# A four-layer graph network on one core: order of the seven products, engine of one product, joined differences, and order at the start of layer 0

## The chip, the cores and the metric

The kernel runs on one core of one Trainium2 chip. A core has engines that each work through their own queue in order: PE (TensorE, the matrix products), DVE (VectorE), ACT (ScalarE), POOL (GpSimd) and SP (SyncE, which here only issues transfers). They meet through semaphores. Matrix products land in PSUM, which this kernel uses as eight banks; everything else lives in SBUF. The metric is the time of one execution in device microseconds (us), and the median of three runs is what versions are compared by.

## The reference

The input `x` has 128 graphs of 64 nodes with 256 features, in float32, and there is one 64x64 adjacency matrix. Four layers follow each other, each `x = x + f(relu(layernorm(x)), adj)`:

```python
# layer 0: two graph convolutions, then an LSTM with windows of 1, 2, 3 and 4 nodes
h = relu(einsum('ts,bsh->bth', adj, x @ Wg0 + bg0))
h = relu(einsum('ts,bsh->bth', adj, h @ Wg1 + bg1))
for p in range(1, 5):                       # own weights for each p
    nw = T // p
    last = lstm_last(Wih[p-1], Whh[p-1], b, h[:, :nw*p].reshape(B*nw, p, H))
    h = h.at[:, arange(nw) * p + (p-1)].set(last.reshape(B, nw, H))
# one LSTM step: g = x_t @ Wih.T + h @ Whh.T + bias; i, f, gg, o = split(g)
#   c = sigmoid(f) * c + sigmoid(i) * tanh(gg);  h = sigmoid(o) * tanh(c)
# layer 1: masked attention; layer 2: graph convolution, two dense layers, batch norm
# layer 3: three times  einsum('nm,bmh->bnh', adj*adj, h @ W)  with relu between
```

In the first step of a window `h` and `c` are zero, so only the product with `Wih` is left and the forget gate isn't needed.

## The kernel before

**Tiling.** The 8192 tokens (graph, node) are cut into 16 groups of 512 (`NG`, tile `[128, 4, 256]`). Adjacency products are done by `mix`: 32 small 64x64 matrix products into two banks, and one copy out of each bank (L146). Wide products in the LSTM and in layer 3 use a scheme of seven half-size products in place of eight.

**Seven products.** `seven` (L153) takes a dictionary of seven products, four banks, and two work tiles `p1` and `p5`. Products 1, 5, 6, 7 go to the four banks; ACT copies the first two banks to `p1` (L162) and `p5` (L163); DVE adds the third bank into `p1` (L165) and the fourth into `p5` (L166). `finish` then lets POOL make block (1,1) from `p1 + p5` (L169), adds product 2 into bank 0 for block (0,0), product 4 into bank 3 for block (1,0), where DVE adds `p1` (L174), and product 3 into bank 1 for block (0,1), where DVE adds `p1` (L177). `end(m, n, ps)` does what follows a block: in the LSTM the gates' activations on ACT (L472), in layer 3 the relu or a copy (L202, L204). In the LSTM `end(1, 0)` acts on both blocks of row 1 at once. Product 4 is added into bank 3 and so comes after that bank's reader, L166; product 3 is added into bank 1 and comes after L163. The operands need sums of one factor's blocks (`sums`, L190) and differences of the other's (`differences`, L182), four instructions each.

**Layer 0, first half.** `first_mix(g)` (L345) normalises group g (`ln_scale`: statistics L91 and L93 on DVE, a power on POOL L95, L97 on DVE; `ln_apply`: L102 on ACT) and mixes it. `first_weights` multiplies with the first weights (L380; DVE adds the bias, L388; POOL's relu, L389), `second_mix` and `second_weights` (L404, L409, L412) follow, as a pipeline over 16 groups. Around the first group stand small setup works: `adjacency_forms` and `normalized_adjacency` on DVE.

**Layer 0, LSTM.** For each window length p the sequences are cut into units; two units are taken together. `first_steps` (L515) does the first time step of both: the differences of each unit's inputs (L184 to L188, 128x256 each), three gate sets with seven products each (input and cell gates of unit 0, output gates of both, input and cell gates of unit 1), then the cell product i * g (`new_cell`, L534, on POOL), its tanh on ACT (L491) and the product with the output gate on DVE (L499, or L493 where another step follows). There are 17 such pairs: 8, 4, 3 and 2 for p = 1 to 4. A gate set's `finish` is put behind the next gate set's first four products by `take`. `next_step` (L549) does the later time steps, a gate set's two halves back to back. The sums of the first-step weights are made by `first_blocks` (L573; L192 to L195 on DVE).

**What sets the order.** The instructions of each engine are put in order when the program is compiled: of those whose operands are ready in a model of the machine, the first in program order is issued next. So order in the source is a wish and not a command. `tc.issue_after(ins)` adds the command that what stands in its block is queued on that instruction's engine behind `ins`, without a wait for it. On the chip each queue is then worked through in that fixed order. All loads of `x` and of the weights go through SP's queue.

Of the kernel before, what the change touches and what calls it, by code (L numbers as in the profile page):

```python
# [8 lines left out]
F32 = mybir.dt.float32  # L9
AF = mybir.ActivationFunctionType  # L10
ALU = mybir.AluOpType
# [3 lines left out]
P = 128  # L15
# [5 lines left out]
NG = NTOK // GN  # L21
GB = GN // NODES
HB = 32
PER = HB // GB
NK = PER
# [13 lines left out]
def adj_preln_kernel(ctx: ExitStack, tc: tile.TileContext, x_in, adj, vec, bg0, bg1,  # L39
                     wg0, wg1, wih, whh, wqkv, w1t, w2t, l3w1, l3w2, l3w3, out):  # L40
    nc = tc.nc
# [111 lines left out]
    def seven(products, banks, p1, p5, out, end):  # L153

        ps = banks
        for i, p in zip((1, 5, 6, 7), ps):  # L160
            products[i](p, True)
        nc.scalar.copy(p1, ps[0])  # L162
        nc.scalar.copy(p5, ps[1])  # L163

        nc.vector.tensor_tensor(p1, p1, ps[2], ALU.add)  # L165
        nc.vector.tensor_tensor(p5, p5, ps[3], ALU.add)  # L166

        def finish():
            nc.gpsimd.tensor_tensor(out=out[1][1], in0=p1, in1=p5, op=ALU.add)  # L169
            end(1, 1, None)  # L170
            products[2](ps[0], False)
            end(0, 0, ps[0])
            products[4](ps[3], False)
            nc.vector.tensor_tensor(out[1][0], p1, ps[3], ALU.add)  # L174
            end(1, 0, None)
            products[3](ps[1], False)
            nc.vector.tensor_tensor(out[0][1], p1, ps[1], ALU.add)  # L177
            end(0, 1, None)

        return finish  # L180

    def differences(eng, b11, b12, b21, b22, t1, t2, t3, t4, negate=False):  # L182

        eng.tensor_tensor(out=t1, in0=b12, in1=b11, op=ALU.subtract)  # L184
        eng.tensor_tensor(out=t3, in0=b22, in1=b12, op=ALU.subtract)
        eng.tensor_tensor(out=t2, in0=b22, in1=t1, op=ALU.subtract)  # L186
        t4a, t4b = (b21, t2) if negate else (t2, b21)
        return eng.tensor_tensor(out=t4, in0=t4a, in1=t4b, op=ALU.subtract).ins  # L188
# [63 lines left out]
    with tc.tile_pool(name="lw", bufs=5) as lw:  # L252
# [6 lines left out]
        with tc.tile_pool(name="gw", bufs=1) as gw, tc.tile_pool(name="gcn", bufs=2) as gp, \  # L259
                tc.tile_pool(name="setup", bufs=1) as sp:  # L260

            load_x(xs[0], 0)
            abd = sp.tile([P, P], F32, tag="abd", name="abd")
            nc.vector.memset(abd, 0.0)
            arow = sp.tile([P, NODES], F32, tag="arow", name="arow")
# [77 lines left out]
            first_copied = None  # L343

            def first_mix(g):  # L345
                nonlocal first_copied
# [24 lines left out]

            def first_weights(m0):
# [52 lines left out]
        with tc.tile_pool(name="back", bufs=1, reuse_waits="tile") as back_pool, \  # L425
                tc.tile_pool(name="diff", bufs=2, reuse_waits="tile") as dp, \
                tc.tile_pool(name="lstm", bufs=2, reuse_waits="tile") as lp:

            def unit(p, tiles, k0, nk):


                n = nk * HB
                win = [
                    hs[i][:, :, k0 * p : (k0 + nk) * p, :].rearrange("p c (k q) b -> p c k q b", q=p)
                    for i in tiles
                ]
                state = lp.tile([P, 2, 2, 2, 256], F32, tag="state", name="state")
                cell, hid = (state[:, i, :, :, 0:n] for i in range(2))
                return lambda t, blk: win[blk][:, :, :, t, :], cell, hid
# [72 lines left out]
                    finish()  # L512
                    then()

            def first_steps(p, n, two, w0):  # L515


                bs = []
                tt = dp.tile([P, 4, 2, 256], F32, tag="diff", name="diff")
                for u, (x_of, _, _) in enumerate(two):  # L520
                    ts = [tt[:, i, u, 0:n] for i in range(4)]
                    x = [[x_of(0, blk)[:, c] for blk in range(2)] for c in range(2)]
                    differences(
                        nc.vector, *x[0], *x[1],
                        *[d.rearrange("p (k b) -> p k b", b=HB) for d in ts], negate=True,
                    )
                    bs.append(([[x[0][0]], None], [[x[1][0]], [x[1][1]]], [[d] for d in ts]))
                igs = [gate_tile() for _ in range(2)]
                both = gate_tile()

                def new_cell(i):
                    def then():
                        gate_i, gate_g = (igs[i][:, r, :, :, 0:n] for r in range(2))
                        nc.gpsimd.tensor_tensor(out=two[i][1], in0=gate_i, in1=gate_g, op=ALU.mult)  # L534
# [12 lines left out]
                take(lambda: gate_set(p, n, igs[1], ig, w0, [bs[1]] * 2), new_cell(1))  # L547
# [43 lines left out]
                return [by_chunk([wx[:, m], wm[:, m]]) for m in range(2)] + [by_chunk(ss)]  # L591


            w0 = first_blocks(w_next[0], lw.tile([P, 2, 1024], F32, tag="w", name="s"))
            for p, nk in ((1, 8), (2, 8), (3, 7), (4, 8)):
                n = nk * HB
                wi, wh = w_next
# [4 lines left out]

                for j in range(0, len(units), 2):
                    two = [unit(p, *u, nk) for u in units[j : j + 2]]
                    first_steps(p, n, two, w0)
                    if p > 1:
                        flush()
                        if j == 0:
# [577 lines left out]
```

## Time and profile before

| what | us |
|---|---|
| runs of this kernel | 2577.28, 2571.56, 2572.81 |
| median of them | 2572.81 |
| the profiled execution | 2576.97 |
| its span in the trace | 2574.9 |
| PE busy in the span | 2492.7 |
| DVE busy | 1457.1 |
| ACT busy | 1132.3 |
| POOL busy | 506.7 |

The span runs from the first to the last instruction; 2.1 us of the profiled execution lie around it. The profiled execution was 4.2 us above the median of the runs. Its mean granted TensorE clock was 0.993. PE's row counts matrix products that overlap, so a mean duration of 370 to 380 ns belongs to products that start about 0.23 us apart (16 of them take 3.73 us on the chain of waits). Every matrix product in the source is two instructions in the trace.

### The profile page before, as it was taken

The page shows a single profiled execution, that of the slowest core. Times are in us where ns is not written, and L with a number is a line of the kernel's source. Part 1 is how long each engine was busy: PE and PEld are TensorE (multiplying, and loading weights), DVE is VectorE, ACT ScalarE, POOL GpSimd, SP SyncE. Part 2 cuts the span into 40 slices and gives each one's busy share as a digit, 9 for nine tenths or more (in the row PEclk, how much of TensorE's full clock was granted, in tenths as well). Part 3 has the DMA queues.
Part 4 walks back from the last instruction along what each step waited for, and adds up shares of the span by engine and source line. Part 5 has one row for each costly group of instructions (what it writes and reads, how often), then busy time and mean ns, then how long its engine had stood idle before and what let it go on. Part 6 is the DMA issues. An engine that isn't in the chain of part 4 may idle for free.

```text
span 2574.9 us, 46812 instructions
## 1 busy us (share of the span) xinstructions
PE 2492.7 (97%) x20184; PEld 2045.8 (79%) x20184; DVE 1457.1 (57%) x2636; ACT 1132.3 (44%) x1982; POOL 506.7 (20%) x384
## 2 busy tenths in 40 slices
PE   6999999999999999999999999998999999999998
PEld 4668778888999998888866664444889889889888
DVE  6547775556555665565466666423645545545544
ACT  3546654444444443344455556472333332332332
POOL 3334432221121121121123221003110110110110
PEclk9999999999999999999999999998999999999999
DMA  4100000001000000000200000001000000000000
GB/s 151 59 2 1 1 17 1 1 1 33 1 1 1 1 1 1 1 29 1 82 2 2 2 18 1 1 21 37 10 9 9 18 10 9 18 9 10 18 9 17
DMA packets 30207, 39.67 MB, mean 15 GB/s; under 512 B 1712, under 2 KB 26416, under 8 KB 30000
## 3 DMA queue, kind: packets, MB, share of 16 engines
q1 hardware_dynamic: 29136, 36.09, 4.2%
q8 instruction: 158, 2.59, 0.4%
q10 hardware_dynamic: 864, 0.59, 0.1%
q14 instruction: 49, 0.40, 0.1%
HBM read 28.29 MB, written 8.39 MB: 14 GB/s over the span
## 4 chain that ended last, share of the span: by engine, by line
PE 80%; DVE 9%; ACT 5%; POOL 3%; issue 2%; DMA 1%; SPq 0%; DVEq 0%; POOLq 0%; ACTq 0%
PE ps L458 29%; PE ps L1010 15%; PE ps L1055 8%; PE ps L690 4%; PE ps L911 4%; PE ps L974 4%; PE ps L134 3%; ACT gates L472 3%; PE ps L663 3%; POOL state L534 2%; PE ps L706 2%; PE ps L380 2%; PE ps L404 2%; ACT gates L491 1%; DVE state L493 1%
## 5 line engine op out<-in xcount | busy, mean ns | idle before, releaser
L458 PE MATMUL ps<-diff,s 128*128 128x256 f32 (+1 forms) x1824 | 397.2, 372 | 13.4 <-DVE diff L561 7.1
L1010 PE MATMUL ps<-arena 128*128 128x256 f32 x1792 | 391.8, 380 | 0.3 <-DVE arena L186 0.2
L458 PEld LDWEIGHTS ps<-diff,s 128*128 128x128 f32 x1824 | 344.8, 190 | 51.6 <-issue 8.9
L1010 PEld LDWEIGHTS ps<-arena 128*128 128x128 f32 x1792 | 338.2, 190 | 53.4 <-issue 7.3
L472 ACT ACTIVATE gates<-gates,lbias 128x512 f32<-128x512 f32 (+4 forms) x426 | 240.5, 619 | 192.1 <-DVE gates L174 166.5
L169 POOL TENSOR_TENSOR gates<-p 128x512 f32<-128x512 f32 (+1 forms) x115 | 154.1, 1340 | 734.0 <-DVE p L166 710.4
L458 PE MATMUL ps<-diff,w 128*128 128x256 f32 (+1 forms) x1040 | 242.0, 374 | 13.5 <-DVE p L166 12.3
L458 PE MATMUL ps<-h,w 128*128 128x256 f32 (+1 forms) x1028 | 241.0, 371 | 0.0
L458 PEld LDWEIGHTS ps<-diff,w 128*128 128x128 f32 x1040 | 196.4, 191 | 37.0 <-DVE p L166 16.4
L458 PEld LDWEIGHTS ps<-h,w 128*128 128x128 f32 x1028 | 194.8, 190 | 18.9 <-issue 0.5
L472 ACT ACTIVATE gates<-ps,lbias 128x256 f32<-128x256 f32 (+3 forms) x213 | 91.4, 476 | 238.3 <-PE ps L458 238.3
L169 POOL TENSOR_TENSOR arena<-arena 128x512 f32<-128x512 f32 x64 | 73.2, 1144 | 540.2 <-DVE arena L166 540.2
L204 ACT ACTIVATE arena<-arena 128x512 f32<-128x512 f32 x144 | 89.4, 630 | 181.5 <-POOL arena L169 103.4
L1055 PE MATMUL ps<-arena 128*128 128x128 f32 x1280 | 153.0, 277 | 1.4 <-DVE arena L192 1.0
L1055 PEld LDWEIGHTS ps<-arena 128*128 128x128 f32 x1280 | 147.0, 192 | 2.9 <-PE ps L1055 1.7
L174 DVE TENSOR_TENSOR gates<-p,ps 128x512 f32<-128x512 f32 (+1 forms) x115 | 76.5, 665 | 119.0 <-PE ps L458 118.6
L165 DVE TENSOR_TENSOR p<-p,ps 128x512 f32<-128x512 f32 (+1 forms) x115 | 76.3, 663 | 101.4 <-PE ps L458 77.1
L174 DVE TENSOR_TENSOR arena<-arena,ps 128x512 f32<-128x512 f32 x64 | 39.8, 621 | 152.2 <-PE ps L1010 84.2
L95 POOL TENSOR_TENSOR rstd<-rstd,mhalf 128x4 f32<-128x4 f32 x64 | 65.4, 1022 | 275.8 <-DVE rstd L94 269.5
L663 PE MATMUL ps<-arena,w 128*128 128x512 f32 x256 | 117.4, 613 | 1.4 <-DVE arena L146 1.3
L458 PE MATMUL ps<-state,s 128*128 128x256 f32 (+1 forms) x512 | 118.0, 374 | 0.0
L458 PE MATMUL ps<-state,w 128*128 128x256 f32 (+1 forms) x512 | 116.0, 370 | 1.4 <-ACT p L162 1.4
(184 smaller groups left out, 4007.7 us busy)
## 6 DMA issues: line engine op xcount, KB each, us to landing
x<-in_x SPq DMA_DIRECT2D x28, 512.0 KB, 5.0
out<-x SPq DMA_DIRECT2D x16, 512.0 KB, 2.9
w<-in_wih SPq DMA_DIRECT2D x4, 1024.0 KB, 9.5
w<-in_whh SPq DMA_DIRECT2D x3, 1024.0 KB, 4.9
arena<-in_l3w SPq DMA_DIRECT2D x3, 1024.0 KB, 5.1
w<-in_wqkv SPq DMA_DIRECT2D x1, 768.0 KB, 4.5
wg<-in_wg ACTq DMA_DIRECT2D x2, 256.0 KB, 3.4
w<-in_w1t SPq DMA_DIRECT2D x1, 512.0 KB, 3.9
```

The source lines that it names most:

```text
L134: nc.tensor.matmul(pss[b][half * 64 : half * 64 + 64, c, t, :], lhsT=src[rows, t, col : col + 64], rhs=a2[rows, :], start=True, stop=True,)
L169: nc.gpsimd.tensor_tensor(out=out[1][1], in0=p1, in1=p5, op=ALU.add)
L174: nc.vector.tensor_tensor(out[1][0], p1, ps[3], ALU.add)
L204: nc.scalar.activation(out[m][n], out[m][n], func)
L458: nc.tensor.matmul(ps[:, r], lhsT=wc[:, j, :], rhs=bc, start=first and r == 0 and c == 0, stop=True, skip_group_check=True,)
L472: nc.scalar.activation(o, ps, func, bias=lbias[:, col : col + 1])
L663: nc.tensor.matmul(ps, lhsT=w1[:, c, m * P : (m + 1) * P], rhs=a[:, 2 + c, :], start=(c == 0), stop=(c == 1),)
L690: nc.tensor.matmul(ps, lhsT=wqk[:, c, col : col + P], rhs=hT[:, c, :], start=(c == 0), stop=(c == 1),)
L911: nc.tensor.matmul(pss[m], lhsT=w2[:, c, m * P : (m + 1) * P], rhs=a[:, c, :], start=(c == 0), stop=(c == 3),)
L974: nc.tensor.matmul(ps[:, t, :], lhsT=w[:, t * P : (t + 1) * P], rhs=b, start=first and t == 0, stop=True, skip_group_check=True,)
L1010: nc.tensor.matmul(ps[:, r, :], lhsT=w[:, c, col : col + P], rhs=b[:, c, :], start=first and r == 0 and c == 0, stop=c == 1, skip_group_ch ...
L1055: nc.tensor.matmul(ps[:, t, :], lhsT=w[:, c, t * P : (t + 1) * P], rhs=b[:, c, :], start=first and t == 0 and c == 0, stop=c == 3, skip_gr ...
```

## The change

Four edits. In `seven`, product 3 and what follows it come before product 4. At the start of layer 0, the load of group 1 is issued right after that of group 0; the statistics of group 1 are queued behind the copies out of group 0's mix, and the setup works and later statistics behind group 1's last statistics instruction; the first call of `first_blocks` is queued behind the copies of group 8's mix. In `first_steps`, the differences of two neighbouring units of the same tiles are made by one set of four instructions over both (two sets remain where the units lie in different tiles, which is the case for one pair of p = 3). The cell product of the first steps goes from POOL to DVE.

```diff
@@ seven @@
             end(0, 0, ps[0])
+            products[3](ps[1], False)
+            nc.vector.tensor_tensor(out[0][1], p1, ps[1], ALU.add)
+            end(0, 1, None)
             products[4](ps[3], False)
             nc.vector.tensor_tensor(out[1][0], p1, ps[3], ALU.add)
             end(1, 0, None)
-            products[3](ps[1], False)
-            nc.vector.tensor_tensor(out[0][1], p1, ps[1], ALU.add)
-            end(0, 1, None)
@@ layer 0 @@
-            load_x(xs[0], 0)
+            for g in range(2):
+                load_x(xs[g], g)
...
-            for g in range(1, NK):
+            for g in range(2, NK):
                 load_x(xs[g], g)
...
-                    with tc.issue_after(first_ln):
+                    with tc.issue_after(first_copied):
                         rstd, nmr, second_ln = ln_scale(xs[1])
                     ln_apply(xs[1], h, rstd, nmr)
-                    with tc.issue_after(second_ln), tc.issue_after(first_copied):
+                    with tc.issue_after(second_ln):
                         adjacency_forms()
                         normalized_adjacency()
...
-                    with tc.issue_after(first_copied):
+                    with tc.issue_after(second_ln):
                         ln_relu(x, h)
...
+                if g == NG // 2:
+                    middle_copied = copied
@@ first_steps @@
-            def first_steps(p, n, two, w0):
+            def first_steps(p, n, two, places, w0):
...
+                (tiles, k0), (tiles_b, k0_b) = places
+                nk = n // HB
+                if tiles == tiles_b:
+
+                    spans = [(k0, 2 * nk, tiles, slice(0, 2))]
+                else:
+                    spans = [(k0, nk, tiles, 0), (k0_b, nk, tiles_b, 1)]
+                for k, span, tls, u in spans:
+                    x = [[windows(p, i, k, span)[:, c, :, 0] for i in tls] for c in range(2)]
+                    ts = [tt[:, i, u, 0:n] for i in range(4)]
...
+                    differences(nc.vector, *x[0], *x[1], *ts, negate=True)
...
-                        nc.gpsimd.tensor_tensor(out=two[i][1], in0=gate_i, in1=gate_g, op=ALU.mult)
+                        nc.vector.tensor_tensor(out=two[i][1], in0=gate_i, in1=gate_g, op=ALU.mult)
...
-            w0 = first_blocks(w_next[0], lw.tile([P, 2, 1024], F32, tag="w", name="s"))
+            with tc.issue_after(middle_copied):
+                w0 = first_blocks(w_next[0], lw.tile([P, 2, 1024], F32, tag="w", name="s"))
```

More of the change, by code (lines that the diff above doesn't have):

```diff
@@ L338, in adj_preln_kernel @@
                 nc.vector.tensor_scalar(rb0[:, 0, :], rb0[:, 0, :], rsum, None, ALU.mult)
-            for g in range(1, NK):
+            for g in range(2, NK):
                 load_x(xs[g], g)
             w_next = (load_w(wih, 0), None)
-            first_copied = None
+            first_copied, middle_copied, second_ln = None, None, None
             def first_mix(g):
-                nonlocal first_copied
+                nonlocal first_copied, middle_copied, second_ln
                 h = gp.tile([P, GT, D], F32, tag="h", name="h")
@@ L427, in adj_preln_kernel, with windows @@
                 tc.tile_pool(name="lstm", bufs=2, reuse_waits="tile") as lp:
+            def windows(p, i, k0, nk):
+                return hs[i][:, :, k0 * p : (k0 + nk) * p, :].rearrange("p c (k q) b -> p c k q b", q=p)
             def unit(p, tiles, k0, nk):
                 n = nk * HB
[L433 to L436, printed above, removed]
+                win = [windows(p, i, k0, nk) for i in tiles]
                 state = lp.tile([P, 2, 2, 2, 256], F32, tag="state", name="state")
@@ L513, in flush @@
                     then()
-            def first_steps(p, n, two, w0):
+            def first_steps(p, n, two, places, w0):
                 bs = []
                 tt = dp.tile([P, 4, 2, 256], F32, tag="diff", name="diff")
+                (tiles, k0), (tiles_b, k0_b) = places
[7 more added lines that the diff above has]
+                    ts = [tt[:, i, u, 0:n] for i in range(4)]
+                    if span > nk:
+                        x = [[b.rearrange("p (u k) b -> p u k b", u=2) for b in row] for row in x]
+                        ts = [d.rearrange("p u (k b) -> p u k b", b=HB) for d in ts]
+                    else:
+                        ts = [d.rearrange("p (k b) -> p k b", b=HB) for d in ts]
+                    differences(nc.vector, *x[0], *x[1], *ts, negate=True)
                 for u, (x_of, _, _) in enumerate(two):
-                    ts = [tt[:, i, u, 0:n] for i in range(4)]
                     x = [[x_of(0, blk)[:, c] for blk in range(2)] for c in range(2)]
-                    differences(
-                        nc.vector, *x[0], *x[1],
-                        *[d.rearrange("p (k b) -> p k b", b=HB) for d in ts], negate=True,
+                    bs.append(
+                        ([[x[0][0]], None], [[x[1][0]], [x[1][1]]], [[tt[:, i, u, 0:n]] for i in range(4)])
                     )
-                    bs.append(([[x[0][0]], None], [[x[1][0]], [x[1][1]]], [[d] for d in ts]))
                 igs = [gate_tile() for _ in range(2)]
@@ L604, in adj_preln_kernel @@
                     two = [unit(p, *u, nk) for u in units[j : j + 2]]
-                    first_steps(p, n, two, w0)
+                    first_steps(p, n, two, units[j : j + 2], w0)
                     if p > 1:
```

## The prediction

> **What bounds the kernel now.** I read the busy times by stage first. The stages are my cuts: start of layer 0, its steady part, LSTM with p = 1, LSTM with p = 2 to 4, layers 1 and 2, start, body and end of layer 3.
>
> ```profile
> core 0: us, PE busy (x) PEld busy (x) DVE busy (x) ACT busy (x) POOL busy (x), PEclk, DMA share, GB/s
> 0.00:60.00 60.00, 36.74 (x526) 26.13 (x527) 39.01 (x140) 20.78 (x35) 20.04 (x23) 0.96 0.46 163
> 60.00:187.00 127.00, 125.17 (x1916) 83.90 (x1914) 64.28 (x149) 62.63 (x93) 45.73 (x34) 0.99 0.10 31
> 187.00:345.00 158.00, 151.03 (x684) 128.80 (x684) 121.38 (x200) 105.30 (x183) 67.43 (x40) 1.00 0.00 1
> 345.00:1270.00 925.00, 903.69 (x4368) 825.21 (x4367) 551.89 (x766) 411.19 (x759) 176.20 (x116) 1.00 0.02 7
> ...
> 1812.00:2555.00 743.00, 742.44 (x7082) 662.31 (x7081) 370.28 (x681) 242.53 (x438) 86.41 (x77) 1.00 0.04 12
> 2555.00:2575.00 20.00, 12.93 (x120) 12.09 (x119) 7.69 (x10) 1.62 (x4) 0.72 (x1) 0.97 0.08 27
> ```
>
> PE is the bound almost everywhere, and the change takes no matrix product away. So it can only win PE's idle time: 23.3 us in the first 60, 7.0 in p = 1, 21.3 in p = 2 to 4, next to nothing in layer 3's body. What PE waits for there is in the groups of the whole page's list:
>
> ```profile
> L458 PE MATMUL ps<-diff,s 128*128 128x256 f32 (+1 forms) x1824 | 397.2, 372 | 13.4 <-DVE diff L561 7.1
> L458 PE MATMUL ps<-diff,w 128*128 128x256 f32 (+1 forms) x1040 | 242.0, 374 | 13.5 <-DVE p L166 12.3
> L458 PE MATMUL ps<-state,w 128*128 128x256 f32 (+1 forms) x512 | 116.0, 370 | 1.4 <-ACT p L162 1.4
> ```
>
> `diff,w` is product 4, and it waits for L166, the reader of its bank. With 13.4 and 1.4 this makes 28.3 us, the most that the LSTM can give. Third, the timeline of the start:
>
> ```profile
> 10.93 1.07 DVE L91 BATCH_NORM_STATS2 st<-x 128x6 f32<-128x256 f32 x3
> 13.61 0.16 DVE L97 SCALAR_TENSOR_TENSOR nmr<-mv,rstd 128x4 f32<-128x4 f32 x1 [1.12 <-POOL rstd L95]
> 16.22 0.69 DVE L192 TENSOR_TENSOR s<-w 128x512 f32<-128x512 f32 x1 [2.44 <-DMA w<-in_wih]
> 16.83 0.68 DVE L194 TENSOR_TENSOR s<-w 128x512 f32<-128x512 f32 x1
> 17.54 1.29 DVE L146 COPY m<-ps 128x512 f32<-128x512 f32 x2
> 18.89 6.34 PE L380 MATMUL ps<-wg,m 128*128 128x256 f32 x16 [7.37 <-DVE m L146]
> ```
>
> The mix of group 0 was done at 11.52, but its two copies L146 stand in DVE's queue behind the statistics of group 1 and behind two sums of LSTM weights, whose transfer lands at 16.22. Fourth, the timeline where a second time step begins:
>
> ```profile
> 435.43 2.85 POOL L534 TENSOR_TENSOR state<-gates 128x1024 f32<-128x1024 f32 x1 [6.37 <-ACT gates L472]
> 438.31 1.06 ACT L491 ACTIVATE gates<-state 128x1024 f32<-128x1024 f32 x1 [2.07 <-POOL state L534]
> 439.40 1.23 DVE L493 TENSOR_TENSOR state<-gates 128x1024 f32<-128x1024 f32 x1 [3.33 <-ACT gates L491]
> 440.55 0.68 DVE L165 TENSOR_TENSOR p<-p,ps 128x512 f32<-128x512 f32 x1
> 441.74 0.68 DVE L166 TENSOR_TENSOR p<-p,ps 128x512 f32<-128x512 f32 x1
> 442.48 1.99 PE L458 MATMUL ps<-diff,w 128*128 128x256 f32 x8 [1.97 <-DVE p L166]
> ```
>
> One chain: cell product on POOL, tanh, product with the output gate; L165 and L166 of the next gate set queue behind it on DVE; product 4 waits 1.97 us.
>
> **What the Trainium skill says.** "PSUM — Partial Sum Buffer", section "Engine vs sequencer instructions", calls the queues of ScalarE, VectorE and GpSimd strict FIFO. The trace agrees: L146 had its data at 11.52 and began at 17.54. "SBUF — State Buffer", section "Who interferes with whom", says that a DVE instruction with two inputs in SBUF contends with a GpSimd instruction that reads SBUF, and that the second one is fully blocked. The trace agrees: L185 at 230.12 took 2.57 us where its median is 0.418, beside an L534 from 229.93 on that took 2.48. "GPSIMD Engine Reference", section "4.1 Engine selection", puts two-input work on GPSIMD at about twice VectorE's time. Here L534 has a median of 2.367 us, and the same shape on DVE (L493, 128x1024) 1.224.
>
> **Start of layer 0.** With the copies queued ahead of the statistics and the sums gone from there, L146 can start at 11.55 and PE's L380 at 12.9, as 1.35 us lay between the two before. 18.89 - 12.9 is 6.0 us. What is late next: group 1's statistics now follow the copies at 12.85; from L91 to the end of L97 they took from 10.33 to 13.77 with an L338 of 0.34 between, so 3.1 us. h of group 1 then comes out of ACT by 18.2. PE works on L380 till 19.2 if it is as slow there as before (6.34 us), so it doesn't wait. The setup works (2 us from 18.75 to 20.5) now stand behind group 1's L97 at 16 and may sit in front of the first L388: I take 0.5 us off. Group 1's transfer is issued ahead of three small ones (vectors and biases); these are first read at 10.68 (L338, before L388 only), so nothing of them is late. ACT's adjacency transfers share the engines with it: they landed by 5.8, and L279 was done at 7.00 with L97 at 7.84, so 0.8 us are free. The four sums L192 to L195 (4 x 0.68 = 2.7 us) go to about 105 us, where DVE is half busy (64.3 of 127) and PE full; without that cover they would cost 2.7. **-5.5**, between -1 (another wait at once in its place) and -7 (DVE freed of L193 and L195 as well).
>
> **Cell product.** 34 times 1.224 on DVE in place of 2.367 on POOL: tanh starts 1.14 us earlier each time. In p = 1 PE waits 0.83 us in almost every pair for L472, which stands on ACT behind L491, which waits for L534 (POOL state L534 made ACT idle 57.0 us over all). Of the 6.98 us of p = 1 I take **-5.0**: the waits for L472 are 5.5, those for L174 (0.15 a pair) stay. DVE's load: 121.4 us over 8 pairs is 15.2 of 19.7 a pair; two cell products add 2.45, joined differences take 8 x 0.418 - 4 x 0.683 = 0.6 off (0.683 is L557's and L561's 128x512), and blocked L184, L185, L188 (means 561, 1192, 499 ns against 419, 418, 414) give back 2.0. So 15.1 to 17.1, under 19.7. At the first gate set of p = 1 the joined L184 takes 0.68 in place of 0.42 with PE waiting: **+0.3**. Where a next step follows, L561 stands behind L493 of unit 0, which is behind the same tanh: four waits of 1.35 to 2.02 shrink by 1.1 each (**-4.4**; one of them was an L195 blocked for 2.84 us by L534).
>
> **Third product ahead of the fourth.** Product 3 needs L163 only, done long before; it lasts 1.8 us in a next step (8 instructions at 0.23) and 0.9 in a first one. In the quoted case product 4 comes at 442.3 and L166 is done at 442.3 even without the quicker cell product, at 441.2 with it. So the waits for L166 go: **-11.7** of 12.3. A gate set's last two activations are now 128x512 instead of 128x256 (2.13 of four either way; later by about 0.4 us), hidden in a step, since the other unit's step (26 us of PE) lies between.
>
> **Layer 3.** At the end, L1055's product 5 waited for L192, which needs block (0,1):
>
> ```profile
> 2556.89 4.48 PE L1055 MATMUL ps<-arena 128*128 128x128 f32 x38 [1.01 <-DVE arena L192]
> 2568.45 1.09 PE L1076 MATMUL ps<-arena,w2s 64*64 64x256 f32 x16 [0.61 <-DVE arena L177]
> ```
>
> (0,1) comes one product (1.7 us) earlier, so the 1.01 goes; half of L1076 can start without the 0.61. **-1.5**. In the body it is the other way round: the second mix begins with (0,0) and (1,0), and (1,0) is now last. Before, it was ready at 2099.3 when PE reached it at 2099.4; now L174 and L204 end near 2100.1. PE would wait up to 0.7 us in 15 groups, 10.5 us, unless other matrix products are put there: the half of the mix that reads (0,1), or the second half of L1076 (0.6 us). Since ready work is issued first, I take **+1.0** (0 to 10.5).
>
> **Sum.** -5.5 - 5.0 + 0.3 - 4.4 - 11.7 - 1.5 + 1.0 = -26.8. Against the profiled execution's 2576.97 (span 2574.9 and 2.1 around it) this is 2550.2; that execution lay 4.2 over the median, so from 2572.81 it is 2546.
>
> **Rivals.** (a) The stall at the start moves, to a sum of the next LSTM weights or to POOL's power: 1 us of gain there, 2550.5. For: DVE is busy 39 of 60 us. Against: those sums stood at 42 us or later before. (b) The second mix stalls in every group: +10.5, 2555.5. For: in layer 3's first group PE idled 0.68 us for an L204. Against: no second half of L1076 exists yet there. (c) The compiled order keeps product 4 ahead: the 12.3 stay, 2558. For: L177 ran ahead of L174 in that same group, so the source doesn't rule. Against: L174 comes first in most gate sets, as the source says. (d) Slower: the cell product waits at the head of DVE's queue for its four activations (2.13 us). DVE's slack in a pair is 19.7 - 17.1 = 2.6 us; two waits of w make a pair longer by 2w - 2.6. With w = 2.13 that is 1.66 in 17 pairs, +28; -5.0 and -4.4 are lost, -17.4 of the rest stay: +10.8, 2584. It decides from w = 1.81. For: POOL waited 75.4 us for ACT before 26 of these products. Against: compiled order puts other DVE work in such a gap.
>
> **How the numbers follow.** Forecast 0.60, (a) 0.10, (b) 0.12, (c) 0.07, (d) 0.11. Low end: all of 28.3, 7 and 1.6 gained, 2536, so 2537. High end 2568 covers (a), (b), (c) and two of them together, leaving (d) out. A measurement of this kernel can tell about 0.2%, 5 us. Faster by more: 0.85; within: 0.05; slower: 0.10.
>
> **What would show it.** L380 should begin near 13; no PE wait for L166 above 0.3 us; POOL's row without `state`; L185 without entries over 1.5 us; L491 waiting for DVE about 1.1 us less; PE idle 187 to 345 near 2. Wrong if DVE idles over 1.8 us before each cell product, or if L134 waits for L204 in every group of layer 3.

## The result, and the profile after

| | before | after |
|---|---|---|
| median of the runs, us | 2572.96 (4 runs) | 2533.81 (4 runs) |
| lowest and highest, us | 2571.56 to 2577.28 | 2533.28 to 2536.0 |
| ratio | | 0.9847, interval 0.983 to 0.9864 |
| span of the profiled execution, us | 2574.9 | 2532.4 |

The changed kernel is 39.2 us faster. 26.8 were forecast, and the lower end of the range was 2537. Line numbers are larger after the change: by 1 from L263 on, by 3 from L370 on, by 16 from L528 on and by 17 from L595 on. L380 is now L383, L458 is L461, L472 L475, L491 L494, L493 L496, L561 L577; the cell product L534 on POOL is L550 on DVE.

First the busy times by stage of the kernel after, with its own stage borders (start of layer 0, its steady part, LSTM with p = 1, LSTM with p = 2 to 4, body of layer 3; the last products of p = 1 come near 326, and the 12 us from there to the border at 338 have no idle time):

```profile
core 0: us, PE busy (x) PEld busy (x) DVE busy (x) ACT busy (x) POOL busy (x), PEclk, DMA share, GB/s
0.00:60.00 60.00, 43.45 (x672) 30.91 (x673) 37.56 (x138) 25.02 (x41) 22.22 (x25) 0.94 0.36 119
60.00:180.00 120.00, 118.11 (x1770) 78.65 (x1768) 66.25 (x152) 58.73 (x89) 43.52 (x31) 0.99 0.16 55
180.00:338.00 158.00, 156.48 (x725) 137.78 (x726) 129.63 (x190) 114.12 (x196) 33.46 (x26) 1.00 0.02 7
338.00:1232.00 894.00, 892.20 (x4336) 818.29 (x4335) 551.64 (x748) 405.30 (x750) 122.17 (x95) 1.00 0.02 5
...
1769.00:2511.00 742.00, 738.73 (x7055) 660.18 (x7054) 367.75 (x671) 240.29 (x436) 86.42 (x77) 1.00 0.04 12
```

In 60 us PE gets through 672 products in place of 526. In p = 1 it idles 1.5 us in place of 7.0, in the longer windows 1.8 in place of 21.3. Layer 3's body, which had 0.6 us of idle, now has 3.3. The groups of the page that answer to the three shown of before:

```profile
L461 PE MATMUL ps<-diff,s 128*128 128x256 f32 (+1 forms) x1824 | 393.5, 371 | 0.9 <-DVE diff L577 0.9
L461 PE MATMUL ps<-diff,w 128*128 128x256 f32 (+1 forms) x1040 | 238.7, 370 | 0.0
L461 PE MATMUL ps<-state,w 128*128 128x256 f32 (+1 forms) x512 | 116.1, 370 | 0.9 <-ACT p L162 0.8
```

28.3 us of idle have become 1.8, and 1.6 more stand at `h,w` (below). All waits for L166 are gone. The timeline of the start:

```profile
11.63 1.29 DVE L146 COPY m<-ps 128x512 f32<-128x512 f32 x2 [2.06 <-PE ps L134]
12.83 1.40 DVE L91 BATCH_NORM_STATS2 st<-x 128x6 f32<-128x256 f32 x4
12.97 5.66 PE L383 MATMUL ps<-wg,m 128*128 128x256 f32 x16 [1.39 <-DVE m L146]
...
22.45 0.33 PE L320 MATMUL ps<-ident,an 128*128 128x128 f32 x1 [3.46 <-DVE an L318]
...
27.50 5.22 PE L383 MATMUL ps<-wg,m 128*128 128x256 f32 x16 [1.92 <-DVE m L146]
```

PE's first weights begin at 12.97 in place of 18.89, with the copies first in DVE's queue. But two waits follow that were much shorter before: 3.46 us for a setup work (L318), where before had 0.32, and 1.92 for group 1's copies, where before had 0.73. Last, the timeline where a second time step begins; the chain is the one shown of before (cell product, tanh, L496, then L165 and L166, product 4):

```profile
413.89 1.22 DVE L550 TENSOR_TENSOR state<-gates 128x1024 f32<-128x1024 f32 x1
415.14 1.06 ACT L494 ACTIVATE gates<-state 128x1024 f32<-128x1024 f32 x1 [0.49 <-DVE state L550]
415.86 0.69 DVE L165 TENSOR_TENSOR p<-p,ps 128x512 f32<-128x512 f32 x1
416.46 1.22 DVE L496 TENSOR_TENSOR state<-gates 128x1024 f32<-128x1024 f32 x1
417.60 0.68 DVE L166 TENSOR_TENSOR p<-p,ps 128x512 f32<-128x512 f32 x1
420.77 1.89 PE L461 MATMUL ps<-diff,w 128*128 128x256 f32 x8
```

L550 takes 1.22 us where L534 took 2.85, L165 now stands ahead of L496, and product 4 comes 2.5 us after L166 is done.

**Where the 42.5 us of the span went.** PE's row has 20184 products in both traces. Setting the time of the k-th of one against the k-th of the other gives, stage by stage (my own sums from the two traces):

| stage | change, us |
|---|---|
| start and steady part of layer 0 | -7.2 |
| LSTM | -35.2 |
| attention and layer 2 | -2.1 |
| layer 3, body | +3.7 |
| layer 3, end | -1.5 |
| sum | -42.3 |

Most of the -2.1 isn't the change's: in that stretch PE's granted clock fell to half twice for 3.4 us in the trace of before and once in that of after, which makes 1.7 (see the unexpected findings). The order of the products accounts for both rows of layer 3: `u_order` and `o_dve`, which have the old order, agree with before in body and end to 0.4 us, and `o_order`, which has only the new one, agrees with after. The profiled execution of before lay 4.2 us above its median, that of after 0.4, so 42.5 stands for about 38.7 between medians; which of these rows holds the 3.8 isn't known.

**The LSTM is where the forecast fell short**, so I counted it in another way. A product of 256 columns starts 0.216 us after the one before where nothing waits (0.189 with 224 columns). What lies between two starts beyond that is lost, whether the profile calls it idle or not:

| lost in the LSTM, us | before | after |
|---|---|---|
| idle that the profile shows | 28.3 | 3.4 |
| time behind these same stops that shows as busy | 5.2 | 1.0 |
| slower first product after a stop, and small rests | 3.5 | 0.6 |
| half clock | 3.2 | 0.0 |
| sum | 40.2 | 4.9 |

The half-clock row comes from two stretches that stand in this trace of before alone; no other kernel's trace has one in the LSTM. Since this execution lay 4.2 us above the median, the row may not hold for a typical one. The second and third row can be read off the timeline of before (columns: start and length in us, the group, idle ahead of it in brackets):

```profile
220.61 1.03 PE L458 MATMUL ps<-h,w 128*128 128x256 f32 x4
221.47 1.03 PE L458 MATMUL ps<-diff,s 128*128 128x256 f32 x4
223.05 1.99 PE L458 MATMUL ps<-diff,s 128*128 128x256 f32 x8 [0.55 <-ACT gates L472]
```

Four products take 0.86 us from start to start (220.61 to 221.47). The next four end with a stop: 223.05 - 221.47 = 1.58, so 0.72 are lost, and the profile shows 0.55. The difference is the last product, whose modelled end lies 0.379 us after its start and not 0.216: every stop hides 0.163 us, however long it is, and 32 stops make 5.2. The eight products after the stop take 1.99 us where eight undisturbed ones take 1.89: the first of them lasts 0.483 us in place of 0.379, and the second starts 0.320 us after it, 0.104 later than usual. So a stop like this one costs the idle that the profile shows and 0.27 us on top.

### The profile page after: what moved, and what is told of

The parts are those of the page before. It is cut to its first block, busy times and chain, and to the rows that moved or that the text cites. A ratio compares the mean times of both kernels' runs of the same rounds, so it can differ in the third digit from the quotient of the medians.

```text
span 2532.4 us, 46818 instructions
## 1 busy us (share of the span) xinstructions
PE 2481.1 (98%) x20184; PEld 2046.5 (81%) x20184; DVE 1462.8 (58%) x2606; ACT 1132.3 (45%) x1982; POOL 418.5 (17%) x350
## 4 chain that ended last, share of the span: by engine, by line
PE 90%; DVE 4%; ACT 2%; POOL 2%; issue 1%; DMA 0%; DVEq 0%; POOLq 0%; ACTq 0%
PE ps L461 40%; PE ps L1027 15%; PE ps L1072 8%; PE ps L707 4%; PE ps L928 4%; PE ps L134 4%; PE ps L680 3%; PE ps L991 3%; PE ps L723 2%; PE ps L383 2%; PE ps L407 2%; POOL rstd L95 1%; DVE st L91 1%; ACT arena L204 1%; PE ps L784 1%
## 5 line engine op out<-in xcount | busy, mean ns | idle before, releaser
L461 PE MATMUL ps<-diff,s 128*128 128x256 f32 (+1 forms) x1824 | 393.5, 371 | 0.9 <-DVE diff L577 0.9
L461 PEld LDWEIGHTS ps<-diff,s 128*128 128x128 f32 x1824 | 345.9, 190 | 33.8 <-issue 1.6
L475 ACT ACTIVATE gates<-gates,lbias 128x512 f32<-128x512 f32 (+5 forms) x426 | 244.1, 620 | 203.6 <-DVE gates L174 146.3
L169 POOL TENSOR_TENSOR gates<-p 128x512 f32<-128x512 f32 (+1 forms) x115 | 148.8, 1294 | 885.1 <-DVE p L166 834.0
L461 PE MATMUL ps<-h,w 128*128 128x256 f32 (+1 forms) x1028 | 241.2, 371 | 1.6 <-ACT p L162 1.6
L461 PE MATMUL ps<-diff,w 128*128 128x256 f32 (+1 forms) x1040 | 238.7, 370 | 0.0
L461 PEld LDWEIGHTS ps<-diff,w 128*128 128x128 f32 x1040 | 197.4, 190 | 18.2
L461 PEld LDWEIGHTS ps<-h,w 128*128 128x128 f32 x1028 | 194.6, 190 | 20.9 <-ACT p L162 2.0
L475 ACT ACTIVATE gates<-ps,lbias 128x256 f32<-128x256 f32 (+3 forms) x213 | 91.8, 477 | 247.0 <-PE ps L461 246.9
L204 ACT ACTIVATE arena<-arena 128x512 f32<-128x512 f32 x144 | 88.1, 628 | 192.4 <-POOL arena L169 103.3
L169 POOL TENSOR_TENSOR arena<-arena 128x512 f32<-128x512 f32 x64 | 73.2, 1144 | 537.9 <-DVE arena L166 537.9
L174 DVE TENSOR_TENSOR gates<-p,ps 128x512 f32<-128x512 f32 (+1 forms) x115 | 76.5, 665 | 119.8 <-PE ps L461 119.8
L461 PE MATMUL ps<-state,w 128*128 128x256 f32 (+1 forms) x512 | 116.1, 370 | 0.9 <-ACT p L162 0.8
L461 PE MATMUL ps<-state,s 128*128 128x256 f32 (+1 forms) x512 | 115.8, 369 | 0.0
L177 DVE TENSOR_TENSOR gates<-p,ps 128x512 f32<-128x512 f32 (+1 forms) x115 | 76.7, 667 | 64.8 <-PE ps L461 64.1
L707 PE MATMUL ps<-hT,w 128*128 128x512 f32 x256 | 112.8, 593 | 0.0
```

The lines of the kernel that those rows point to most:

```text
L204: nc.scalar.activation(out[m][n], out[m][n], func)
L461: nc.tensor.matmul(ps[:, r], lhsT=wc[:, j, :], rhs=bc, start=first and r == 0 and c == 0, stop=True, skip_group_check=True,)
L475: nc.scalar.activation(o, ps, func, bias=lbias[:, col : col + 1])
L707: nc.tensor.matmul(ps, lhsT=wqk[:, c, col : col + P], rhs=hT[:, c, :], start=(c == 0), stop=(c == 1),)
```

## The experiments

Every kernel was measured beside runs of the kernel before on its own chip (median of these: 2577.1 for the first four, 2573.96 for the next four, 2577.32 for `u_sums` and `u_stats`, 2576.73 for the last two).

| kernel | what it is | median, us | ratio and interval | span, us |
|---|---|---|---|---|
| u_order | after, product 4 first again | 2533.36 | 0.9833 (0.9819 to 0.9848) | 2532.7 |
| u_pool | after, cell product on POOL | 2548.07 | 0.9891 (0.9876 to 0.9905) | 2546.3 |
| u_split | after, differences apart | 2532.77 | 0.9832 (0.9815 to 0.9848) | 2529.9 |
| u_start | after, start of layer 0 as before | 2543.32 | 0.9872 (0.9857 to 0.9887) | 2540.4 |
| o_order | before, product 3 first | 2561.90 | 0.9946 (0.9928 to 0.9964) | 2560.5 |
| o_dve | before, cell product on DVE | 2541.61 | 0.9869 (0.9853 to 0.9885) | 2540.1 |
| a_again | after, unchanged | 2534.68 | 0.9843 (0.9827 to 0.9858) | 2532.4 |
| best1 | see below | 2528.13 | 0.9817 (0.9801 to 0.9832) | 2527.0 |
| u_sums | after, sums not held back | 2545.62 | 0.9876 (0.986 to 0.9893) | 2544.5 |
| u_stats | after, statistics placed as before | 2532.49 | 0.9827 (0.9812 to 0.9841) | 2530.3 |
| best1_again | best1, unchanged | 2527.26 | 0.9807 (0.9794 to 0.9821) | 2526.0 |
| best2 | best1 with u_stats' edit | 2527.72 | 0.9811 (0.9797 to 0.9824) | 2524.6 |

### Which edit of the LSTM gave the 35 us

The prediction has two gains that add: 11.7 us from the order of the products and 9.4 from the cell product. The rival is that both cut the same chain, so that one of them alone brings most. Each edit was undone alone, and done alone.

```diff
 # u_order, in seven: the kernel after with product 4 first; o_order is the reverse edit on the kernel before
-            products[3](ps[1], False)
-            nc.vector.tensor_tensor(out[0][1], p1, ps[1], ALU.add)
-            end(0, 1, None)
             products[4](ps[3], False)
             nc.vector.tensor_tensor(out[1][0], p1, ps[3], ALU.add)
             end(1, 0, None)
+            products[3](ps[1], False)
+            nc.vector.tensor_tensor(out[0][1], p1, ps[1], ALU.add)
+            end(0, 1, None)
```

> The changed kernel with product 4 ahead of product 3 again, everywhere. Theory W (the waits and what each stop hides add up, and most of the LSTM's gain is the quicker cell product): the waits for L166 come back shortened, some 0.9 us at seven places with 0.16 us of restart each, so the LSTM is 5 to 9 us longer; layer 3's body gets some 4 us shorter and its end 1.5 longer; together 2537 to 2541. Rival Q (the order of the products is the main cause): all 12.3 us of waits for L166 come back with their restarts and half-clock stretches, LSTM 14 to 18 us longer, 2546 to 2550.

> The kernel before with product 3 ahead of product 4 and nothing else. Theory S (the order and the quicker cell product each remove the waits for L166 by themselves, so that neither is missed much when only it is undone): PE's visible wait for L166 falls from 12.3 us to under 0.5, the stretch with p = 1 stays as it was, and the run is 12 to 20 us quicker, 0.992 to 0.995 of the time before. Rival C (the cell product alone did it, the order nothing): 10 us or more of the waits for L166 stay, ratio 0.998 to 1.002.

```diff
 # u_pool, in new_cell: the kernel after; o_dve is the reverse edit on the kernel before
-                        nc.vector.tensor_tensor(out=two[i][1], in0=gate_i, in1=gate_g, op=ALU.mult)
+                        nc.gpsimd.tensor_tensor(out=two[i][1], in0=gate_i, in1=gate_g, op=ALU.mult)
```

> The changed kernel with the cell product of the first steps on POOL again. Theory W: the stretch with p = 1 is 11 to 13 us longer, as its losses of before return; in p = 2 to 4 the waits for L561 return (7) and those for L166 do not, as product 3 covers them; 2551 to 2555. Rival Q: only the 9.4 us of the prediction return, 2543.

> The kernel before with the cell product of the first steps on DVE and nothing else. Theory S: lost time of PE in the LSTM falls from 40 us to between 6 and 9, the waits for L166 to about 1 us, though product 4 still comes ahead; ratio 0.986 to 0.989. The prediction's own steps: 12 us of waits for L166 stay and only 9.4 go, ratio 0.996. The slower rival of the prediction (DVE waits at its head for the four activations): DVE idle 1.8 us before each cell product, ratio above 1.

What PE waited for in the whole LSTM, as the view of the waits has it (us in total, times, longest; the lines left out of o_order and u_pool sum to 1.1 and 2.4 us in the LSTM). o_order:

```profile
PE ps L458 <- ACT gates L472: 12.0, 7, 1.7
PE ps L458 <- DVE diff L561: 5.7, 4, 1.6
...
```

o_dve:

```profile
PE ps L458 <- DVE p L166: 1.1, 4, 0.3
PE ps L458 <- ACT p L162: 0.9, 2, 0.6
PE ps L458 <- DVE diff L184: 0.5, 1, 0.5
PE ps L458 <- DVE diff L561: 0.5, 2, 0.3
```

u_pool:

```profile
PE ps L461 <- ACT gates L475: 5.8, 7, 0.8
PE ps L461 <- DVE diff L577: 5.7, 4, 1.6
...
```

Before had 12.3 us in 10 waits for L166 and 7.1 in 4 for L561 from 345 us on. Both edits take the waits for L166 away, each by itself: the order to nothing, the cell product to 1.1 us. Only the cell product takes the others, for the activations and for the differences. Counted from start to start as above, the LSTM loses 40.2 us before, 22.9 in o_order, 5.6 in o_dve and 4.9 after. So the cell product alone is worth 34.6 us there, the order alone 17.2 (both with the 3.2 of half clock that only before's trace has), and once the product is on DVE the order adds 1.7 (u_order loses 6.6). The medians of the whole kernel agree in kind: o_dve gains 32.4 us, o_order 12.1, after 39.3 (as a_again). In the whole kernel the order adds nothing to the cell product: u_order and the kernel after have the same ratio within their intervals, since layer 3 gives the 1.7 back (below). The rival held. In the other two runs the sizes expected were too large: u_order came out 3.6 us below the 2537 to 2541 expected of it, and u_pool 2.9 below 2551 to 2555.

Why is the cell product worth more than its 1.14 us of shorter work? In o_dve, at the place that the prediction quoted of before, the chain reads:

```profile
420.39 1.22 DVE L534 TENSOR_TENSOR state<-gates 128x1024 f32<-128x1024 f32 x1
...
422.30 0.69 DVE L165 TENSOR_TENSOR p<-p,ps 128x512 f32<-128x512 f32 x1
422.91 1.22 DVE L493 TENSOR_TENSOR state<-gates 128x1024 f32<-128x1024 f32 x1
423.76 1.89 PE L458 MATMUL ps<-state,w 128*128 128x256 f32 x8
424.04 0.68 DVE L166 TENSOR_TENSOR p<-p,ps 128x512 f32<-128x512 f32 x1
```

L166 ends 0.96 us after the product with `state` begins; before it ended 3.80 after it (442.42 against 438.62). Of these 2.84 us, 1.63 are the shorter cell product (2.85 to 1.22, more than the medians' 1.14, because L534 was slower on this chain than in the median) and the other 1.2 are in the main the compiled order: L165 runs ahead of L493 and no L558 stands ahead of L166 any more.

o_order also shows a price that the forecast had only for later steps, as 0.4 us and hidden. At p = 1 its seven stops for the activations are 1.6 to 1.7 us long where before had 0.55 to 0.83. Its timeline ahead of one:

```profile
216.40 0.67 DVE L174 TENSOR_TENSOR gates<-p,ps 128x512 f32<-128x512 f32 x1
216.62 1.27 POOL L169 TENSOR_TENSOR gates<-p 128x512 f32<-128x512 f32 x1 [2.83 <-DVE h L499]
216.99 1.18 DVE L188 TENSOR_TENSOR diff<-h,diff 128x256 f32<-128x256 f32 x1
218.09 0.67 DVE L177 TENSOR_TENSOR gates<-p,ps 128x512 f32<-128x512 f32 x1
218.80 1.33 ACT L472 ACTIVATE gates<-gates,lbias 128x512 f32<-128x512 f32 x2 [0.79 <-DVE gates L177]
```

The compiled order put a difference, L188, between the two additions of the gate set; it took 1.18 us in place of 0.42 beside POOL's L169 (the contention that the Trainium skill describes in "SBUF — State Buffer", section "Who interferes with whom"). ACT waits 0.79 us, the cell product begins 1.42 us before PE's next set in place of 2.50, and its tanh and the activations behind it are as much later. In the kernel before the two additions stood back to back. The new order of the products need not cost this: u_pool has it too, with the differences joined, and its stops for the activations are at most 0.8 us.

**Rival (d), DVE as the new bound.** In the kernel after, DVE did wait for the activations at the head of its queue before L550, 18.6 us in 15 of 34 cases, 1.24 each in the mean and 1.9 at most; the mean is below the 1.81 from which this was to decide. PE doesn't notice: a pair of p = 1 takes 18.13 us, which is its 84 products at 0.216.

### The start of layer 0

The prediction credited two commands together, the copies ahead of the statistics and the sums of the LSTM weights held back; the question is which of them brings the gain. u_start undid the whole part, u_sums only the command on the sums, u_stats only the loads and the statistics.

```diff
 # u_sums; u_start is this together with u_stats
-            with tc.issue_after(middle_copied):
-                w0 = first_blocks(w_next[0], lw.tile([P, 2, 1024], F32, tag="w", name="s"))
+            w0 = first_blocks(w_next[0], lw.tile([P, 2, 1024], F32, tag="w", name="s"))
```

```diff
 # u_stats
-            for g in range(2):
-                load_x(xs[g], g)
+            load_x(xs[0], 0)
...
-                    with tc.issue_after(first_copied):
+                    with tc.issue_after(first_ln):
                         rstd, nmr, second_ln = ln_scale(xs[1])
...
-                    with tc.issue_after(second_ln):
+                    with tc.issue_after(second_ln), tc.issue_after(first_copied):
                         adjacency_forms()
...
-                    with tc.issue_after(second_ln):
+                    with tc.issue_after(first_copied):
                         ln_relu(x, h)
```

> The changed kernel with the start of layer 0 as it was before: load of group 1 behind the small loads, its statistics ahead of the copies, the sums of LSTM weights free. Theory W: the start up to the LSTM is 7 to 9 us longer, all of it before 65 us of the span, and nothing changes after it; 2541 to 2543. Rival: the gain there is the 5.5 us of the prediction and the rest is from elsewhere, 2539.

> The changed kernel without the command that keeps the first sums of LSTM weights (L192 to L195) behind group 8. If these sums and the transfer that they wait for were the stop at the start: two of them stand ahead of the copies of group 0 again, PE's first L383 begins near 17 to 19 instead of 13, 4 to 6 us of the start's gain are lost, 2538 to 2540. If the statistics of group 1 were the stop: under 1.5 us lost, 2534 to 2536.

> The changed kernel with group 1's load and statistics where they were before (ahead of group 0's copies), the sums of LSTM weights still behind group 8. If the sums were the stop: the copies wait for the end of the statistics at 13.8 only, L383 begins near 15, 2 us lost at first and at most 3 at 65 us, 2535 to 2537. If the statistics were: 5 us or more lost.

All of the gain is the command on the sums: u_sums' span is 12.1 us longer than that of the kernel after, u_stats' 2.1 shorter (1.7 of that a half-clock stretch less). Both went beyond what was expected of them: u_sums was put at 2538 to 2540 and measured 2545.6, u_stats at 2535 to 2537 and measured 2532.5, which its interval doesn't tell from the kernel after. u_start came within 0.4 us of its range. u_sums' timeline shows what happens when the copies are only ahead of the statistics:

```profile
16.96 0.69 DVE L192 TENSOR_TENSOR s<-w 128x512 f32<-128x512 f32 x1 [7.84 <-DMA w<-in_wih]
...
18.28 1.29 DVE L146 COPY m<-ps 128x512 f32<-128x512 f32 x2
...
19.63 5.10 PE L383 MATMUL ps<-wg,m 128*128 128x256 f32 x16 [8.14 <-DVE m L146]
```

DVE stands 7.84 us at L192 for a transfer, with finished work behind it. In u_stats the first weights begin at 15.52 and not 12.97, and yet by the 600th product it is 1.0 us ahead: the 2.5 us are given back in the two later waits (3.46 and 1.92 after, 1.15 and 0.73 in u_stats). Two executions of the kernel after differ by 0.6 us there (a_again), so the 1.0 says little.

With the command on the sums, more moves than the sums themselves. SP's queue in the kernel before, the first of three loads of later weights (the others at 14.26 and 15.17):

```profile
12.97 1.25 SPq L256 DMA_DIRECT2D w<-in_wih  x1
```

and in the kernel after (the others at 95.28 and 95.83):

```profile
85.71 0.51 SPq L256 DMA_DIRECT2D w<-in_wih  x1
```

The compiled order has these loads behind nine loads of `x` now; why it put them there isn't shown. With them went five of the seven sums that DVE of before made between 42 and 55 us; the other two, of the first weights, are held back by the command itself. Before in that stretch:

```profile
51.32 0.46 PE L134 MATMUL ps<-adj,h 64*64 64x64 f32 x16 [1.33 <-POOL h L389]
53.40 1.21 DVE L194 TENSOR_TENSOR s<-w 128x1024 f32<-128x1024 f32 x1
53.80 0.93 PE L134 MATMUL ps<-adj,h 64*64 64x64 f32 x48 [2.02 <-POOL h L389]
54.53 1.28 DVE L146 COPY m<-ps 128x512 f32<-128x512 f32 x2
55.87 4.63 PE L380 MATMUL ps<-wg,m 128*128 128x256 f32 x10 [1.14 <-DVE m L146]
```

Between the 440th and the 540th product PE of before lost 6.8 us against after: in these waits, and at half clock from 54.9 on. u_start has the same waits (1.32 and 2.02) and a half-clock stretch; u_stats has 0.29 and 0.99, and none. So three quarters of the stage's 9.0 us came here, and the prediction saw only the stall at 16 us, of which 2.2 us were left by the 440th product. u_sums makes its sums as early, though, with waits of at most 0.8 us there; it had lost its 11.7 us before. What the sums cost thus depends on what else stands late at the time.

### Joined differences

```diff
 # u_split, in first_steps
-                if tiles == tiles_b:
+                if False:
```

> The changed kernel with the differences of the two units made separately again, four 128x256 instructions each. Theory W: DVE has room in p = 1, so nothing changes, 2533 to 2535, and the first gate sets of p = 1 are up to 0.5 us quicker. Rival: the joined differences are what lets DVE keep up in p = 1, which gets 3 to 6 us longer, 2537 to 2540.

The first gate set of p = 1 in the kernel after:

```profile
181.52 0.70 PE L461 MATMUL ps<-h,w 128*128 128x256 f32 x2 [1.60 <-ACT p L162]
```

PE idles 1.60 us there, for ACT's copy L162, and 0.54 with the differences apart, for the difference L184: the joined ones cost 1.06, not 0.3. With them the compiled order puts two products `h,w`, which wait for that copy, ahead of the first ones with `diff`. The rest of the LSTM is the same to 0.02 us. The time can't tell the two apart (intervals overlap).

### The same program again, and a mixed order

best1 keeps product 4 first in the first of layer 3's three weights, where block (1,0) starts the second mix, and the differences apart. best2 adds u_stats' edit.

```diff
 # best1, with the edit of u_split
-    def seven(products, banks, p1, p5, out, end):
+    def seven(products, banks, p1, p5, out, end, four_first=False):
...
+            for part in (fourth, third) if four_first else (third, fourth):
+                part()
...
-            blocks, ends_in(blocks, AF.Relu),
+            blocks, ends_in(blocks, AF.Relu), four_first=True,
```

> The changed kernel once more, as it is, on the chip of these runs. If the half-clock stretches of 3.4 us behind stops of about 1.8 us come by the phase of a window that the program doesn't set, they stand elsewhere than at 173.9 and 1518.8 in this trace, and its span differs by 1.7 us or a multiple of it in one or two places and by under 0.3 us elsewhere. If they belong to the stops, they are where they were.

> The changed kernel with two edits: layer 3's first weights take product 4 ahead of product 3 again, as the second mix begins with block (1,0), and the differences of the two units are made separately. Expected from the runs before: layer 3's body 3 to 5 us shorter (11 waits of 0.26 for L204 with their restarts), the first gate set of p = 1 about 1 us shorter; 4 to 6 us quicker than the changed kernel, ratio to before 0.981 to 0.983. If the waits for L204 only cover others, the body stays within 1 us.

> The same program as best1, on the same chip as best2. If its profile differs from that of best1 only by where half-clock stretches lie, its span is 2527.0 within 1.7 us. Theory of independent parts: about 1 us slower than best2; rival: 2.5 us quicker than it.

> best1 with the edit of u_stats added: product 4 first again in layer 3's first weights, differences apart, x of group 1 loaded and its statistics placed as in the kernel before; the sums command, the DVE cell product and the third product first in the LSTM stay. Theory that the parts are independent and that the copies-ahead-of-statistics edit costs about 1 us at the start: span 1.0 us shorter than that of best1 (2527.0), so near 2526, apart from one half-clock stretch more or less (1.7 us). Rival, that best1's gain was tied to its own order at the start, for example because the earlier copies are needed when the sums come later: L383 comes at 15.5 us in place of 13 and the 2.5 us stay, span 2529.5.

In layer 3's body of the kernel after, nearly every group (they come 48 us apart) has a line like this one:

```profile
2054.13 1.74 PE L134 MATMUL ps<-w2s,arena 64*64 64x64 f32 x104 [0.26 <-ACT arena L204]
```

PE reaches block (1,0) before its relu L204 is done: 3.1 us over 12 waits in all of layer 3, and some time lost around each stop. best1 has no such wait. Its median is 6.6 us below that of the kernel after on the same chip, a little more than the 4 to 6 expected; in the traces layer 3's body gives 4.8 of it and the first gate set of p = 1 1.1. best2's span is 1.4 us shorter than that of best1_again, which fits independent parts (1.0 expected), but the medians are the same (2527.72 and 2527.26), so the copies ahead of the statistics neither help nor harm measurably. best1 is the version to keep.

## Why the prediction was right or wrong, point by point

**What bounds the kernel: right, with a wrong ceiling.** PE was the bound and only its idle time could be won. But "28.3 us, the most that the LSTM can give" was wrong: 40.2 us were lost there before, and 35.2 came back, where the sum of the forecast's LSTM terms is 20.8. This is the step that put the measured time outside the range. The idle column leaves out up to 0.27 us around each stop, and the pace I had taken, 16 products in 3.73 us, held the modelled end of the last one and a restart. From start to start the pace is 0.216, and a pair's 19.65 us against 84 x 0.216 = 18.1 would have shown the loss as 1.5 us a pair, where the idle column has 0.98 (0.83 and 0.15).

**Cell product, -5.0, -4.4 and order, -11.7: the sum too small, its split wrong.** In visible idle 20.8 net were forecast and 24.9 measured; 4.2 more lay behind the stops, 2.9 mostly in slow first products after them, and 3.2 in half-clock stretches that after doesn't have there. The order was credited with the waits for L166, which the cell product removes by itself to 1.1 us. "Even without the quicker cell product" was right as far as it went: o_order shows it. That the reverse holds too was not worked out. The price of the order, put at 0.4 us "hidden in a step", left out p = 1: there the cell product starts 1.1 us later, on PE's path, when the order is changed alone.

**Joined differences, +0.3: 1.06.** The forecast had PE wait for the longer L184. It waits for L162 there, as the compiled order of the products has changed.

**Start, -5.5: -9.0 by the 600th product, -7.2 at the stage's end** after a half-clock stretch that costs 1.75. L380's (L383's) start at 12.9 was right to 0.1 us, and it took both commands (15.52 with the sums alone, 19.63 with the placement alone). But what the placement gained was lost again at once: the setup works, priced at 0.5 us, cost a wait of 3.46, and that PE would not wait for group 1 was wrong (1.92). The gain that stayed came with the sums at 42 us, which I used as evidence against a moved stall and did not price. That the stage's -7.2 lies near the forecast's -5.5 is in part luck, as the new waits and the gain that wasn't priced pull opposite ways.

**Layer 3, -1.5 and +1.0: -1.5 and +3.7.** The end was right: no wait is left in it. In the body neither extreme came: a wait in nearly every group, but 0.26 us and not 0.7.

**Rivals.** (a) The stall did move, to waits of 5.4 us, but far more was gained elsewhere. (b) came at a third of its price. (c) is excluded: in after's trace product 3 (`h,s` or `state,s`) runs directly ahead of product 4 (`diff,w`) in 86 of 88 gate sets, and no wait for L166 is left. (d) is refuted above: w is 1.24 in 15 cases. Of the other signs named, L185's longest is 0.69 us, and ACT waits 15.2 us for the cell product in place of 57.0, 1.2 less each time.

## What to carry to other kernels

Count lost time on the bounding engine from start to start of its instructions against the pace of an undisturbed stretch, not from the idle column: with many short stops the column left out 12 us of 40 here, 3.2 of them at half clock. When two edits both shorten the chain ahead of one wait, work out each as if the other were already made; here the second was worth 1.7 us in place of 17.2. When a command holds work back, look at what else the compiled order moves with it: here three loads went too, with everything made from them, and most of the gain of that stage came from there.

## What the hardware showed that I had not expected

**Half clock after short stops.** PE's granted clock falls to 0.5 for 3.4 us, or a multiple, at moments that differ from one execution of a program to the next. Two executions of the same program, the kernel after and a_again, both with a span of 2532.4, between 160 and 180 us:

```profile
160.00:180.00 20.00, 18.11 (x171) 10.11 (x169) 5.93 (x10) 7.42 (x10) 3.12 (x3) 0.91 0.00 1
```

```profile
160.00:180.00 20.00, 16.92 (x172) 9.78 (x170) 7.62 (x13) 8.61 (x11) 3.63 (x3) 1.00 0.00 1
```

Both have the same stop of 1.8 us at L407 ahead of it; only in the first is it followed by a half-clock stretch (0.91 in the mean). Near 1520 the first has one of 3.4 us, the second one of 6.8. The Trainium skill, "TensorE: Matmul & The Clock Gate", section "What's actually happening", has half rate after an idle window of about 3.4 us that runs freely. The length of 3.4 us agrees; the stops that it follows here and in before's LSTM (1.8 and twice 2.0 us) are shorter than a window. Why one stop is followed by half clock and the next not stays open; a stretch of 3.4 us costs about 1.7 (an estimate: half of its length), so spans of single executions can't settle less than that.

**A stop costs 0.24 to 0.27 us more than its idle.** An f32 product of 256 columns is 0.379 us long in the profile, while products follow each other every 0.216 us, so 0.163 us of each stop look busy; and the first product after a stop is slower: by 0.104 us (0.483) in 26 of the 32 stops of before's LSTM, by 0.075 in the six that wait for L184 or L561. All 32 show both.
